# Turning a normalised activation by VectorE and DRAM instead of TensorE, in a two-layer graph network on one core

## The chip, the cores and the metric

The kernel runs on one NeuronCore of a Trainium2 chip. The metric is the device time of one execution in microseconds. One core has five engines with queues of their own: TensorE (PE in the profile; its weight loads are listed apart as PEld), VectorE (DVE), ScalarE (ACT), GpSimd (POOL) and SyncE (SP), which here only issues DMAs. [...]

## The reference, cut to what matters

There are 32 graphs of 512 nodes with 512 features and one adjacency matrix for all of them. Layer 0 mixes neighbours and adds the result to x, then normalises. Layer 1 is masked attention with 8 heads, added and normalised again.

```python
# layer 0
mi = einsum('bkd,od->bko', x, Wi);  mj = einsum('bkd,od->bko', x, Wj)
h  = layernorm(x + deg[None, :, None] * (mi + b) + einsum('ij,bjo->bio', a, mj))
# layer 1
q, k, v = (split_heads(h @ W.T + bias) for W, bias in ((Wq, bq), (Wk, bk), (Wv, bv)))
s    = where(adj == 0, -inf, (q @ k.T) / sqrt(64))
attn = softmax(s) @ v
out  = layernorm(h + attn @ Wo.T + bo)
```

All of it is float32. The three products with Wq, Wk and Wv need h with the features on the partitions, while the normalisation of layer 0 needs it with the nodes on the partitions. So h has to be turned once for each graph. This turning is what the change is about.

## The kernel before, in words

**Names.** For graph b, `XT[b]` is x, later h, later the output: four chunks of 128 nodes by 512 features. `XD[b]` is x turned and multiplied by the degree, `AX_T[b]` the gathered neighbours turned, `HT[b]` h turned. `TX`, `TA`, `TH` and `TO` hold sums of quarters of `XD`, `AX_T`, `HT` and of the attention's output `OT`. All of these but `XT` and `OT` are tiles named `big`, of which there are six.

**Products in seven pieces.** Each 512x512x512 product is done by Strassen's scheme (Winograd's form): seven products of quarters, numbered 1 to 7 (L366 to L436). Pieces 1, 2 and 3 take plain quarters of the activation; 5, 6, 7 and 4 take the sums t1, t2, t3 and t4, which GpSimd makes by subtracting (`combos`, L353 to L362). Pieces share a PSUM bank within a group: 1 and 2, then 6, 7 and 4, then 5 and 3. There are five products for a graph: `l0` (two weights, so each piece is double), `v`, `q`, `k`, and `pj`, the output projection. After a piece, ScalarE or VectorE adds the bank's content to where it belongs. Two banks, a and b, are used in turn, so a piece waits until the piece two before it has been taken away.

**Weights.** The weights' quarters come from DRAM into a ring of eight tiles. After each piece the next tile's load is written on SP's queue (L257 to L262). It can be issued only when the piece has freed its tile, and SP does nothing else in the meantime.

**Order of the work.** Everything is written out by hand as lists of pieces. For each graph n there is a list of phase b (the rest of `l0` of graph n mixed with `pj` of graph n-2), phase c (`v`, `q` and part of `k` of graph n) and phase a (gathers of graph n+1 with the rest of `k` of graph n). `by_steps` cuts it into eight steps of equal TensorE cost, by costs written in the code. Ahead of each step's pieces go the scores and the values of the attention of graph n-1 (L441 to L467) and, in every second step, the sums of the softmax. The softmax's own follow-up (reciprocals, scaling) and some partial sums are handed out after the pieces, one for each 1.73 of written cost. Entries of cost zero, as statistics, scalings, loads and combinations, stand in the lists where their instructions are to be written on their engines.

**Normalising and turning h before.** `stats` (VectorE L274, L275, then three small operations of GpSimd, L276 to L278) and `apply` (ScalarE, L281) each take half the nodes. `l0_norm` (L332 to L339) then turns one chunk of 128 nodes: four TensorE transposes into a PSUM tile that is otherwise used for scores, and one ScalarE copy to `HT`. It stands four times in each graph's lists, with a written cost of 0.44.

**Turning x.** From graph 1 on, x isn't turned by TensorE. `load_xa` (L105 to L110) loads x from DRAM with four DMAs whose runs are 32 floats, so that the 32x32 blocks lie where their turned form belongs. `l0_turn` (L320 to L325) then turns the blocks by VectorE's transpose and multiplies by the degree on GpSimd. The tile `xa` exists once.

Of the kernel before, what the change touches and what calls it, by code (L numbers as in the profile page):

```python
# [9 lines left out]
FT = mybir.dt.float32  # L10
# [15 lines left out]
def gnn_attention_kernel(  # L26
# [51 lines left out]
    def work(shape, name, bufs, dtype=FT):  # L78
        return pools.work.tile(shape, dtype, name=name, bufs=bufs)
# [13 lines left out]
    def turn_tile():  # L93


        return sc_tile()[:, 0, :]

    XT, XA, XD, AX_T, HT, MV = {}, {}, {}, {}, {}, {}
    QT, KT, V, OT = {}, {}, {}, {}
    TX, TA, TH, TO = {}, {}, {}, {}  # L100

    def rows(ap):
        return ap.rearrange("(c p) d -> p c d", p=P)
# [228 lines left out]
    def l0_norm(b, ic):  # L332
# [5 lines left out]
            nc.tensor.transpose(pt[:, dc * P:(dc + 1) * P], y[:, dc * P:(dc + 1) * P], ident)  # L338
        nc.scalar.copy(HT[b][:, :, ic * P:(ic + 1) * P], pt.rearrange("p (c i) -> p c i", c=DC))  # L339

    def add_bo(b, half):
        for ic in range(2 * half, 2 * half + 2):
            y = XT[b][:, ic, :]
            nc.gpsimd.tensor_add(y, y, bo_r)


    def quarter(src, j, n):
        return src[:, 2 * j:2 * j + 2, Q * n:Q * n + Q]
# [28 lines left out]
    def piece(kind, b, i, bank):  # L377
        g = GROUP[i]
        first = (kind, b, g) not in OPEN
        if first:  # L380
            OPEN[kind, b, g] = mm_tile(bank)
        pm = OPEN[kind, b, g]
        terms = []
        for name, (quarters, T) in zip(NAMES[kind], sources(kind, b)):
            a = {1: (0, 0), 2: (1, 0), 3: (1, 1)}.get(i)
            terms.append((take((name, i)), quarters(*a) if a else T[:, {5: 0, 6: 1, 7: 2, 4: 3}[i]]))
        for c in range(2):
            for n, (w, t) in enumerate(terms):
                for kc in range(2):
                    cut = slice(c * P, (c + 1) * P)  # L390
                    lhs, rhs = (w[:, kc, cut], t[:, kc, :]) if kind in "qk" else (t[:, kc, cut], w[:, kc, :])

                    nc.tensor.matmul(pm[:, c * Q:(c + 1) * Q], lhs, rhs, start=first,  # L393
                                     stop=(kc == 1 and n == len(terms) - 1), skip_group_check=True)
                    first = False
        prefetch()
        pm = pm.rearrange("p (c i) -> p c i", c=2)
        if i == 1:
            p1 = OPEN[kind, b, "p1"] = work([P, 2, Q], "p1", 3)
            nc.scalar.copy(p1, pm)  # L400
        p1 = OPEN[kind, b, "p1"]
        f, n = {1: (0, 0), 2: (0, 0), 6: (0, 1), 3: (0, 1), 4: (1, 0), 7: (1, 1), 5: (1, 1)}[i]
        if kind in ("l0", "pj"):
            y = XT[b]
            if i == 1:
                for n, f in ((1, 0), (1, 1), (0, 1)):
                    d = quarter(y, n, f)
                    nc.gpsimd.tensor_tensor(d, d, p1, op=OP.add)  # L408
            else:
                d = quarter(y, n, f)  # L410
                nc.vector.tensor_tensor(d, d, pm, op=OP.add)
        elif kind == "v":
            if i == 1:
                V[b] = work([P, NC, D], "v", 2)
            d = quarter(V[b], n, f)
            if i == 2:
                nc.scalar.copy(d, pm)
            elif i in (6, 7, 4):
                nc.vector.tensor_tensor(d, pm, p1, op=OP.add)  # L419
            elif i != 1:  # L420
                nc.vector.tensor_tensor(d, d, pm, op=OP.add)
        else:
            T, bias = (QT, bq_c) if kind == "q" else (KT, bk_c)
            if i != 1 and (b, f) not in T:
                T[b, f] = work([P, 2, N], kind, 3)
            if i in (6, 7):
                nc.vector.tensor_tensor(T[b, f][:, :, Q * n:Q * n + Q], pm, p1, op=OP.add)  # L427
            elif i != 1:
                for c in range(2):
                    d = T[b, f][:, c, Q * n:Q * n + Q]  # L430
                    bc = bias[:, 2 * f + c:2 * f + c + 1]
                    if i == 2:
                        nc.scalar.activation(d, pm[:, c, :], AF.Identity, bias=bc, scale=1.0)
                    else:
                        o = p1[:, c, :] if i == 4 else d
                        nc.vector.scalar_tensor_tensor(d, pm[:, c, :], bc, o, op0=OP.add, op1=OP.add)  # L436


    E, ES, PV, RL = {}, {}, {}, {}
# [71 lines left out]
    def z(f, *a):  # L511
        return (0.0, f, *a)

    def pc(kind, b, i, bank):
        return (2 * PC if kind == "l0" else PC, piece, kind, b, i, bank)

    ORDER = (1, 2, 6, 7, 4, 5, 3)
    ALONE = ((1, "a"), (6, "b"), (2, "a"), (7, "b"), (5, "a"), (4, "b"), (3, "a"))

    def banks(n):  # L520

        return ("a", "b") if n % 2 == 0 else ("b", "a")

    def phase_a(n):

        A, K = banks(n)
        if n == B:
            return [pc("k", n - 1, i, bank) for i, bank in ((6, K), (7, K), (5, A), (4, K), (3, A))]
        xq, aq = lambda j, m: quarter(XD[n], j, m), lambda j, m: quarter(AX_T[n], j, m)
        g = [(GA, l0_gather, n, dc, A) for dc in range(DC)]  # L530
        k = [pc("k", n - 1, i, K) for i in ORDER[2:]]
        res = []
        for i in range(DC):
            res += g[i:i + 1] + k[i:i + 1]
            if n + 1 < B:
                res += [z(load_xa, n + 1, i)]
            if n == 1 and i in (1, 3):
                res += [z(combine, "wo", nc.vector, i // 2)]
            if i == 1:
                res += [z(combos, TX, n, xq, (1,)), z(combos, TA, n, aq, (1,))]  # L540
        return res + [z(combos, TX, n, xq, (2,)), z(combos, TA, n, aq, (2,)), z(base, n, 0),
                      z(combos, TX, n, xq, (3, 4)), z(combos, TA, n, aq, (3, 4)), z(base, n, 1),
                      pc("l0", n, 1, A), k[4]]
# [36 lines left out]
    def phase_b(n):  # L580

        m = n - 2
        if m < 0:
            res = []
            side = [z(add_bo, 0, i) for i in range(2)]
            A, K = banks(n)
            for i, bank in ((2, A), (6, K), (5, A), (7, K), (4, K), (3, A)):
                res.append(pc("l0", n, i, bank))
                if i == 4:
                    res += [z(stats, n, 0)]  # L590
                res += side[:1]
                side = side[1:]
            return res + [z(apply, n, 0), z(stats, n, 1), (TR, l0_norm, n, 0), (TR, l0_norm, n, 1)]
        res = project(m, 1)
        for i in ORDER[1:]:
            res.append(pc("l0", n, i, banks(n)[0]))
            if i == 4:
                res.append(z(stats, n, 0))
            if i == 5:
                res.append(z(stats, m, 0))  # L600
            if i == 3:
                res += [z(stats, n, 1), (TR, l0_norm, n, 1)]
            res += project(m, i)
            if i == 4:
                res.append(z(apply, n, 0))
            if i == 5:
                res.append((TR, l0_norm, n, 0))
            if i in (7, 4):
                res.append(z(add_bo, n - 1, int(i == 4)))
        return res  # L610

    def phase_c(n):

        m = n - 2
        norm = [(TR, l0_norm, n, ic) for ic in range(NC)]
        h = lambda j, i: quarter(HT[n], j, i)
        A, K = banks(n)
        res = [pc("v", n, 1, A)] + ([z(apply, n, 1)] if n else []) + [pc("q", n, 1, K)]
        if m >= 0:
            res += [z(stats, m, 1)]  # L620
        res += [pc("v", n, 2, A), norm[2], norm[3], z(combos, TH, n, h, (1, 2)), pc("k", n, 1, A),
                z(combos, TH, n, h, (3, 4)), pc("q", n, 2, K), pc("k", n, 2, A)]
        side = []
        if n == 0:

            side = [z(graph_forms, 2), None, z(graph_forms, 0), None, z(graph_forms, 1)]
        if m >= 0:
            res += [z(apply, m, 0), z(apply, m, 1), z(store, m)]
        for i in ORDER[2:]:
            for f in pc("q", n, i, K), pc("v", n, i, A):  # L630
                res += [f] + [g for g in side[:1] if g]
                side = side[1:]
            if i == 7 and 0 < n < B - 1:
                res += [z(load_x, n + 1)]
            if n + 1 < B and i != 3:
                res += [z(l0_turn, n + 1, (6, 7, 4, 5).index(i))]
            if i == 5 and n + 1 < B:
                res += [z(ahead, n + 1)]
        return res

# [266 lines left out]
```

## Time and profile before

| | us |
|---|---|
| median of 14 runs | 3837.95 (3834.87 to 3841.58) |
| profiled execution | 3836.23 |
| its span on the core | 3834.4 |
| TensorE busy | 3794.9 (99%) |
| VectorE busy | 2586.8 (67%) |
| GpSimd busy | 1990.8 (52%) |
| ScalarE busy | 1064.0 (28%) |
| DMA engines, mean share in the queue of SP's loads and stores | 43.0% |
| h's transposes on TensorE, L338, x512: busy | 73.5 (mean 276 ns) |
| copies of these on ScalarE, L339, x128: busy | 72.0 (mean 592 ns) |
| VectorE's transposes of x, L324, x124: busy | 85.6 (mean 690 ns) |
| granted TensorE clock, share of full speed | 0.997 |

The span runs from the first to the last instruction in the profile. Busy times of matmuls overlap one another, so the cost of a TensorE instruction in a dense stretch is better read as the distance between starts. The run has 32 graphs, and the steady part repeats every 117.7 us.

### The profile page before, as it was taken

What the parts mean: (1) busy time and instruction counts of PE and PEld (TensorE: products, weight loads), DVE (VectorE), ACT (ScalarE), POOL (GpSimd) and SP (SyncE); (2) the same over time, 40 slices, a digit from 0 to 9 for tenths busy, and PEclk for the clock granted to TensorE, in tenths of its full rate; (3) what the DMA queues carried; (4) which work ended last, traced back from release to release, by engine and by line L of the source; (5) the groups of instructions that cost most, each with busy time, mean ns of one, the idle gap of its engine ahead of it and who ended that gap; (6) DMA issues with size and microseconds to landing.
All of it is one profiled execution on the core that took longest, in us unless ns stands there. A gap on an engine that the chain in (4) does not pass through costs nothing.

```text
span 3834.4 us, 46277 instructions
## 1 busy us (share of the span) xinstructions
PE 3794.9 (99%) x16906; PEld 2593.8 (68%) x16906; DVE 2586.8 (67%) x3520; ACT 1064.0 (28%) x1476; POOL 1990.8 (52%) x1985
## 2 busy tenths in 40 slices
PE   9999999999999999999999999999999999999997
PEld 6666767666667666666666666767676767666663
DVE  4667676666767676666767676676667676666765
ACT  2232232222232223322223322232222232222222
POOL 4555554555545555445555455554555554555523
PEclk9999999999999999999999999999999999999998
DMA  8434444444444344434444443444434444444330
GB/s 254 127 99 130 126 121 124 124 109 122 126 123 129 99 129 122 129 118 114 119 128 121 126 124 105 126 124 124 127 99 129 127 121 125 125 108 122 115 111 29
DMA packets 537798, 466.33 MB, mean 122 GB/s; under 512 B 279008, under 2 KB 375776, under 8 KB 537568
## 3 DMA queue, kind: packets, MB, share of 16 engines
q1 hardware_dynamic: 537312, 462.78, 43.0%
q8 instruction: 138, 2.26, 0.3%
q14 instruction: 92, 0.75, 0.1%
q0 software_dynamic: 256, 0.53, 0.0%
HBM read 421.80 MB, written 41.42 MB: 121 GB/s over the span
## 4 chain that ended last, share of the span: by engine, by line
PE 95%; DVE 3%; DMA 1%; issue 0%; ACT 0%; POOL 0%; SPq 0%; POOLq 0%; DVEq 0%; ACTq 0%
PE mmb L393 30%; PE mma L393 30%; PE sc L445 12%; PE ov L466 12%; PE mmb L310 3%; PE mma L310 3%; PE ov L473 3%; PE sc L338 1%; DVE e L450 1%; DVE rl L488 1%; DVE st L274 0%; ACT sc L449 0%; DVE es L458 0%; PE ov L483 0%; DMA wq<-e 0%
## 5 line engine op out<-in xcount | busy, mean ns | idle before, releaser
L449 ACT ACTIVATE sc<-sc 128x1024 f32<-128x1024 f32 x512 | 492.9, 1007 | 1354.2 <-PE sc L445 1350.0
L450 DVE TENSOR_TENSOR e<-sc,edge 128x1024 f32<-128x1024 f32 x512 | 602.4, 1217 | 374.7 <-ACT sc L449 374.7
L393 PE MATMUL mmb<-ring,big 128*128 128x256 f32 x3144 | 728.5, 380 | 0.2 <-ACT big L339 0.2
L393 PE MATMUL mma<-ring,big 128*128 128x256 f32 x3112 | 721.3, 380 | 2.8 <-DVE v L419 1.1
L393 PEld LDWEIGHTS mmb<-ring,big 128*128 128x128 f32 x3144 | 593.3, 190 | 106.0 <-issue 25.9
L393 PEld LDWEIGHTS mma<-ring,big 128*128 128x128 f32 x3112 | 587.0, 190 | 108.6 <-issue 25.6
L362 POOL TENSOR_TENSOR big<-big 128x512 f32<-128x512 f32 x376 | 524.9, 1424 | 205.5 <-ACT big L316 164.9
L445 PE MATMUL sc<-q,k 64*128 64x512 f32 x2048 | 509.7, 616 | 0.0
L466 PE MATMUL ov<-e,v 128*64 128x512 f32 x2048 | 496.0, 605 | 5.8 <-DVE oT L498 5.7
L488 DVE RECIPROCAL rl<-ov 128x128 f32<-128x128 f32 x512 | 459.2, 927 | 15.4 <-PE ov L473 6.0
L393 PE MATMUL mma<-big,ring 128*128 128x256 f32 x1808 | 434.3, 383 | 1.3 <-DVE k L436 0.2
L393 PE MATMUL mmb<-big,ring 128*128 128x256 f32 x1776 | 427.0, 383 | 2.0 <-DVE k L427 0.8
L276 POOL TENSOR_SCALAR mv<-mv 128x1 f32<-128x1 f32 x256 | 49.5, 193 | 724.1 <-DVE mv L275 713.9
L325 POOL TENSOR_TENSOR big<-big,deg_r 128x512 f32<-128x512 f32 x124 | 157.5, 1270 | 512.3 <-DVE big L324 512.3
L393 PEld LDWEIGHTS mma<-big,ring 128*128 128x128 f32 x1808 | 336.9, 190 | 83.5 <-issue 24.3
L393 PEld LDWEIGHTS mmb<-big,ring 128*128 128x128 f32 x1776 | 330.5, 190 | 84.7 <-issue 26.0
L466 PEld LDWEIGHTS ov<-e,v 128*64 128x64 f32 x2048 | 124.6, 136 | 345.9 <-issue 270.8
L456 POOL TENSOR_TENSOR es<-e 128x1024 f32<-128x1024 f32 x128 | 302.0, 2359 | 76.7 <-PE ov L473 63.7
L458 DVE TENSOR_TENSOR es<-es,e 128x1024 f32<-128x1024 f32 x248 | 319.3, 1288 | 0.0
L445 PEld LDWEIGHTS sc<-q,k 64*128 64x128 f32 x2048 | 176.6, 186 | 208.1 <-issue 208.1
L193 POOL TENSOR_TENSOR xlo<-xh,xhi 128x512 fp32r<-128x512 f32 x128 | 163.5, 1288 | 213.9 <-ACT xhi L192 213.9
L408 POOL TENSOR_TENSOR xh<-xh,p 128x512 f32<-128x512 f32 x186 | 231.9, 1275 | 45.8 <-ACT sc L449 39.0
(147 smaller groups left out, 3702.8 us busy)
## 6 DMA issues: line engine op xcount, KB each, us to landing
ring<-wq SPq DMA_DIRECT2D x160, 256.0 KB, 2.7
ring<-wv SPq DMA_DIRECT2D x160, 256.0 KB, 2.7
ring<-wk SPq DMA_DIRECT2D x160, 256.0 KB, 2.8
ring<-wi SPq DMA_DIRECT2D x155, 256.0 KB, 2.8
ring<-wj SPq DMA_DIRECT2D x155, 256.0 KB, 2.7
ring<-wo SPq DMA_DIRECT2D x155, 256.0 KB, 2.6
xh<-in_x_dram SPq DMA_DIRECT2D x32, 1024.0 KB, 5.4
xa<-in_x_dram SPq DMA_DIRECT2D x124, 256.0 KB, 3.8
```

The source lines that it names most:

```text
L193: nc.gpsimd.tensor_sub(lo, xs, hi.bitcast(FT))
L310: nc.tensor.matmul(pm, parts[w][:, jc, :], adjR[:, jc, :], start=(w == 0 and jc == 0), stop=(w == 1 and jc == NC - 1))
L362: nc.gpsimd.tensor_tensor(dst, p, q, op=OP.subtract)
L393: nc.tensor.matmul(pm[:, c * Q:(c + 1) * Q], lhs, rhs, start=first, stop=(kc == 1 and n == len(terms) - 1), skip_group_check=True)
L408: nc.gpsimd.tensor_tensor(d, d, p1, op=OP.add)
L445: nc.tensor.matmul(ps[:, s, :], KT[b, hp // 2][r, hp % 2, kc * P:(kc + 1) * P], QT[b, hp // 2][r, hp % 2, :], start=True, stop=True)
L449: nc.scalar.activation(ps, ps, AF.Exp, scale=QSCALE)
L450: nc.vector.tensor_tensor(e, ps, edge[:, kc:kc + 1, :].to_broadcast([P, 2, N]), op=OP.mult)
L456: nc.gpsimd.tensor_add(ES[hp], E[0], E[1])
L458: nc.vector.tensor_add(ES[hp], ES[hp], E[half])
L466: nc.tensor.matmul(PV[hp][s * HD:(s + 1) * HD, :], V[b][:, kc, c0:c0 + HD], E[kc][:, s, :], start=(kc == 0), stop=(kc == NC - 1))
L488: nc.vector.reciprocal(rl[:, c], pl[:, c])
```

## The change

For graphs 2 to 31, h is turned in the way x already was. There are two halves of 256 nodes. For each half:

1. `h_store`: ScalarE issues a DMA that writes the normalised half of `XT` to a DRAM tile (two of these in turn);
2. `h_load`: SP issues four DMAs that read it back in runs of 32 floats into the tile `xa`, so that the 32x32 blocks lie in place;
3. `h_turn`: VectorE turns the half's blocks in one instruction, from `xa` into `HT`.

Graphs 0 and 1 keep `l0_norm`. As the tile `xa` now serves x and h, x's loads move from phase a of the graph before to phase c of the graph before, behind pieces 6 and 7 of q and v, and `l0_turn` moves from phase c to phase a, one behind each gather and piece of k. The load of x in plain form stands behind piece 3 now.

The order of the pieces is different. Phase b starts with a piece of `l0`, not of `pj`, and `pj` piece 3 has moved to phase c. In phase c, for graphs 2 to 31, the first pieces are v1, pj3, v2, q1, k1, q2, k2. The rest of q, v and k is done as 5, 3, 6, 7, 4 instead of 6, 7, 4, 5, 3. So the first piece that lands in a quarter is now 5 or 3 where it was 6 or 7, and the additions of `piece` follow this: the first adds the kept product 1 (and the bias), later ones add to what is there. The number of additions is the same.

```diff
+    def h_store(b, half):
+        if half == 0:
+            HR[b] = dram.tile([N, D], FT, name="hd", bufs=2)
+        nc.scalar.dma_start(rows(HR[b])[:, 2 * half:2 * half + 2, :], XT[b][:, 2 * half:2 * half + 2, :])
+
+    def h_load(b, half):
+        if half == 0:
+            HA[b] = work([P, DC, N], "xa", 1).rearrange("p (n c) (d i) -> p n (c d) i", n=2, d=2)
+        src = HR[b].rearrange("(t p) (c q f) -> q p c t f", p=32, q=4, f=32)
+        for q in range(4):
+            nc.sync.dma_start(HA[b][32 * q:32 * q + 32, half].rearrange("p c (t f) -> p c t f", f=32),
+                              src[q][:, :, 8 * half:8 * half + 8, :])
+
+    def h_turn(b, half):
+        if half == 0:
+            HT[b] = big()
+        nc.vector.transpose(HT[b][:, :, Q * half:Q * half + Q], HA[b][:, half])
...
+    LATE = (5, 3, 6, 7, 4)
...
-        k = [pc("k", n - 1, i, K) for i in ORDER[2:]]
+        k = [pc("k", n - 1, i, K) for i in LATE]
         res = []
         for i in range(DC):
-            res += g[i:i + 1] + k[i:i + 1]
-            if n + 1 < B:
-                res += [z(load_xa, n + 1, i)]
+            res += g[i:i + 1] + k[i:i + 1] + [z(l0_turn, n, i)]
...
+        A = banks(n)[0]
+        l0 = {i: pc("l0", n, i, A) for i in ORDER}
+        return [l0[2], *project(m, 1), l0[6], *project(m, 2), l0[7], z(add_bo, n - 1, 0), *project(m, 6), l0[4], z(stats, n, 0),
+                *project(m, 7), z(apply, n, 0), z(h_store, n, 0), l0[5], z(h_load, n, 0), z(add_bo, n - 1, 1), *project(m, 4),
+                l0[3], z(stats, n, 1), z(h_turn, n, 0), *project(m, 5)]
...
+            res = [z(apply, n, 1), z(h_store, n, 1), v[1], *project(m, 3), z(h_load, n, 1), z(stats, m, 0), v[2], z(stats, m, 1),
+                   q[1], k[1], z(apply, m, 0), q[2], z(apply, m, 1), z(store, m), z(h_turn, n, 1),
+                   z(combos, TH, n, h, (1, 2)), z(combos, TH, n, h, (3, 4)), k[2]]
...
+        for i in LATE:
+            for f in q[i], v[i]:
                 res += [f] + [g for g in side[:1] if g]
                 side = side[1:]
-            if i == 7 and 0 < n < B - 1:
+                if i in (6, 7) and 0 < n < B - 1:
+                    res += [z(load_xa, n + 1, 2 * (i == 7) + (f is v[i]))]
+            if i == 3 and 0 < n < B - 1:
                 res += [z(load_x, n + 1)]
-            if n + 1 < B and i != 3:
-                res += [z(l0_turn, n + 1, (6, 7, 4, 5).index(i))]
-            if i == 5 and n + 1 < B:
+            if i == 7 and n + 1 < B:
                 res += [z(ahead, n + 1)]
```

More of the change, by code (lines that the diff above doesn't have):

```diff
@@ L96, in turn_tile @@
         return sc_tile()[:, 0, :]
+    HA, HR = {}, {}
     XT, XA, XD, AX_T, HT, MV = {}, {}, {}, {}, {}, {}
@@ L411, in piece @@
                 nc.vector.tensor_tensor(d, d, pm, op=OP.add)
-        elif kind == "v":
-            if i == 1:
[L414 to L424, printed above, removed]
-                T[b, f] = work([P, 2, N], kind, 3)
[L426 to L436, printed above, removed]
@@ new lines, in piece @@
+        else:
+            new = (kind, b, f, n) not in OPEN
+            OPEN[kind, b, f, n] = True
+            if kind == "v":
+                if i == 1:
+                    V[b] = work([P, NC, D], "v", 2)
+                d = quarter(V[b], n, f)
+                if i == 2:
+                    nc.scalar.copy(d, pm)
+                elif i != 1:
+                    nc.vector.tensor_tensor(d, pm, p1 if new else d, op=OP.add)
+                return
+            T, bias = (QT, bq_c) if kind == "q" else (KT, bk_c)
+            if i == 1:
+                return
+            if (b, f) not in T:
+                T[b, f] = work([P, 2, N], kind, 3)
+            d = T[b, f][:, :, Q * n:Q * n + Q]
+            if i != 2 and not new:
+                nc.vector.tensor_tensor(d, pm, d, op=OP.add)
+                return
+            for c in range(2):
+                bc = bias[:, 2 * f + c:2 * f + c + 1]
+                if i == 2:
+                    nc.scalar.activation(d[:, c], pm[:, c, :], AF.Identity, bias=bc, scale=1.0)
+                else:
+                    nc.vector.scalar_tensor_tensor(d[:, c], pm[:, c, :], bc, p1[:, c, :], op0=OP.add, op1=OP.add)
@@ L527, in phase_a @@
         if n == B:
-            return [pc("k", n - 1, i, bank) for i, bank in ((6, K), (7, K), (5, A), (4, K), (3, A))]
+            return [pc("k", n - 1, i, bank) for i, bank in ((6, K), (5, A), (7, K), (3, A), (4, K))]
         xq, aq = lambda j, m: quarter(XD[n], j, m), lambda j, m: quarter(AX_T[n], j, m)
         g = [(GA, l0_gather, n, dc, A) for dc in range(DC)]
-        k = [pc("k", n - 1, i, K) for i in ORDER[2:]]
+        k = [pc("k", n - 1, i, K) for i in LATE]
         res = []
         for i in range(DC):
-            res += g[i:i + 1] + k[i:i + 1]
-            if n + 1 < B:
-                res += [z(load_xa, n + 1, i)]
+            res += g[i:i + 1] + k[i:i + 1] + [z(l0_turn, n, i)]
             if n == 1 and i in (1, 3):
@@ L593, in phase_b @@
             return res + [z(apply, n, 0), z(stats, n, 1), (TR, l0_norm, n, 0), (TR, l0_norm, n, 1)]
[L594 to L610, printed above, removed]
+        A = banks(n)[0]
[3 more added lines that the diff above has]
+                l0[3], z(stats, n, 1), z(h_turn, n, 0), *project(m, 5)]
     def phase_c(n):
@@ L617, in phase_c @@
         A, K = banks(n)
[L618 to L622, printed above, removed]
+        v, q, k = [{i: pc(kind, n, i, bank) for i in ORDER} for kind, bank in (("v", A), ("q", K), ("k", A))]
+        if m < 0:
+            res = [v[1]] + ([z(apply, n, 1)] if n else []) + [q[1], v[2], norm[2], norm[3], z(combos, TH, n, h, (1, 2)), k[1],
+                                                             z(combos, TH, n, h, (3, 4)), q[2], k[2]]
+        else:
+            res = [z(apply, n, 1), z(h_store, n, 1), v[1], *project(m, 3), z(h_load, n, 1), z(stats, m, 0), v[2], z(stats, m, 1),
+                   q[1], k[1], z(apply, m, 0), q[2], z(apply, m, 1), z(store, m), z(h_turn, n, 1),
+                   z(combos, TH, n, h, (1, 2)), z(combos, TH, n, h, (3, 4)), k[2]]
         side = []
@@ L626, in phase_c @@
             side = [z(graph_forms, 2), None, z(graph_forms, 0), None, z(graph_forms, 1)]
[L627 to L630, printed above, removed]
+        for i in LATE:
+            for f in q[i], v[i]:
                 res += [f] + [g for g in side[:1] if g]
                 side = side[1:]
-            if i == 7 and 0 < n < B - 1:
+                if i in (6, 7) and 0 < n < B - 1:
+                    res += [z(load_xa, n + 1, 2 * (i == 7) + (f is v[i]))]
+            if i == 3 and 0 < n < B - 1:
                 res += [z(load_x, n + 1)]
-            if n + 1 < B and i != 3:
-                res += [z(l0_turn, n + 1, (6, 7, 4, 5).index(i))]
-            if i == 5 and n + 1 < B:
+            if i == 7 and n + 1 < B:
                 res += [z(ahead, n + 1)]
```

## The prediction

> **What bounds the kernel now.** I read the page's busy shares and chain first, then TensorE's timeline over one graph, then VectorE's and GpSimd's around the joints that the change moves, and the DMA issues last. The page:
>
> ```profile
> span 3834.4 us, 46277 instructions
> ...
> PE 3794.9 (99%) x16906; PEld 2593.8 (68%) x16906; DVE 2586.8 (67%) x3520; ACT 1064.0 (28%) x1476; POOL 1990.8 (52%) x1985
> ...
> PE 95%; DVE 3%; DMA 1%; issue 0%; ACT 0%; POOL 0%; SPq 0%; POOLq 0%; DVEq 0%; ACTq 0%
> ```
>
> TensorE is the chain. It never pauses visibly, so what leaves it shortens the run unless a new wait appears. TensorE's timeline (start, duration, line, operation, tiles):
>
> ```profile
> 1913.35 1.89 PE L393 MATMUL mma<-ring,big 128*128 128x256 f32 x8
> 1915.34 1.99 PE L393 MATMUL mmb<-big,ring 128*128 128x256 f32 x8
> 1917.17 1.89 PE L393 MATMUL mma<-ring,big 128*128 128x256 f32 x8
> 1918.90 1.04 PE L338 MATMUL sc<-ident,xh 128*128 128x128 f32 x8
> 1919.78 1.96 PE L393 MATMUL mma<-big,ring 128*128 128x256 f32 x8
> ...
> 2021.05 0.60 PE L338 MATMUL sc<-ident,xh 128*128 128x128 f32 x4
> 2021.48 3.62 PE L393 MATMUL mmb<-ring,big 128*128 128x256 f32 x16
> 2025.03 1.99 PE L445 MATMUL sc<-q,k 64*128 64x512 f32 x8
> 2026.95 1.94 PE L466 MATMUL ov<-e,v 128*64 128x512 f32 x8
> 2028.82 0.66 PE L338 MATMUL sc<-ident,xh 128*128 128x128 f32 x4
> ```
>
> Durations overlap, so starts are to be subtracted: a single piece costs 1.73 us (1917.17 to 1918.90), an l0 piece 3.46 to 3.55, scores 1.92, values 1.87. The L338 transposes cost 0.88, 0.43 and (next start 2029.32) 0.50: 1.81 us a graph. The distance from the transposes at 1903.35 to those at 2021.05 gives the period, 117.70 us. A piece of v to a piece of q at 1913.35 takes 1.99, not 1.73: 0.26 of a hidden wait for a bank. Two q and v starts near 1948 add 0.3 in the same way, where VectorE turns x.
>
> VectorE (three rows) and then GpSimd (one), for scores that start at 1936.87:
>
> ```profile
> 1939.08 2.36 DVE L450 TENSOR_TENSOR e<-sc,edge 128x1024 f32<-128x1024 f32 x2 [0.75 <-ACT sc L449]
> 1941.35 0.70 DVE L324 STREAM_TRANSPOSE big<-xa 128x512 f32<-128x512 f32 x1
> 1942.68 0.88 DVE L436 SCALAR_TENSOR_TENSOR q<-mmb,bq_c,p 128x256 f32<-128x256 f32 x2 [0.63 <-PE mmb L393]
> ```
>
> ```profile
> 1942.13 1.27 POOL L325 TENSOR_TENSOR big<-big,deg_r 128x512 f32<-128x512 f32 x1 [5.14 <-DVE big L324]
> ```
>
> An operation queued behind the two masks e starts 4.48 us after its step's scores; GpSimd follows a transpose's end by 0.08. The DMA table:
>
> ```profile
> xh<-in_x_dram SPq DMA_DIRECT2D x32, 1024.0 KB, 5.4
> xa<-in_x_dram SPq DMA_DIRECT2D x124, 256.0 KB, 3.8
> out_dram<-xh SPq DMA_DIRECT2D x31, 1024.0 KB, 5.2
> ```
>
> [...] no DRAM round trip of this kind is in the trace. [...] with xa alone in flight the engines move about 210 GB/s, about 390 with 2 KB rows.
>
> **The change part by part**, per graph; 30 graphs (2 to 31) take the new way, graphs 0 and 1 keep TensorE's transposes.
>
> Removed: 16 transposes on TensorE, 1.81 us; 30 times is 54.3 us. Four L339 copies on ScalarE (4 x 0.59 = 2.4 us) were hidden.
>
> Added: two stores of 512 KB issued by ScalarE. Nearest rows: the SP store of 1 MB, issue 0.39, landing 5.2; 256 KB stores at the end landed in 2.0; so 512 KB about 3.1 (bounds 2.0 and 5.2). ScalarE's own issue could cost 0.3 to 2.0 (the shortest and longest ring issue on SP); I take 0.4. ScalarE is 28% busy and has just given up 2.4 us.
>
> Two times four loads of 128 KB by SP. xa's issue is 0.59 for twice the size; I keep 0.65 with the gap, 2.6 us for four. Landing of the last: 3.1 (bounds 2.5 and 5, as xa spread 3.5 to 5.0). Both halves move 1 MB at 210 GB/s plus 1 MB stored at 390: 5.0 + 2.7 = 7.7 us of DMA on a share of 0.45, which becomes about 0.5.
>
> Two transposes of 128x1024 on VectorE. 512 elements take 0.70; [...] twice the row is 1.40. I take 1.25.
>
> **First half.** T is the end of l0[4]. The order written by the lists, cut in eight steps, is: pj7; scores, values, sums (1.92+1.78+0.96); l0[5], pj4, l0[3], pj5; scores, values; v1. So v1 comes at T+20.9. Exponentials of that step's scores end 3.1 after they start, T+4.9; two L281 of 0.78 end at T+6.5, with statistics ready at about T+4. Store issued T+6.6, landed T+9.7. SP reaches h_load only behind the ring tiles that l0[5]'s end frees, T+10.1; last landing 10.1+2.0+3.1 = T+15.2. VectorE reaches h_turn at T+15.4 (l0[3]) + 0.61 add + 0.87 reciprocal + 0.61 scale + 1.66 stats = T+19.15. It doesn't wait for the DMA, with 4.0 to spare. It ends at T+20.4: 0.4 ahead of v1. Queued behind h_turn are pj5's addition, tell and the next two masks; a late h would stop these too, and through v1 TensorE itself. Ring tiles queued on SP behind h_load are delayed by about 1 to 2 us, against a lead of eight tiles, at least four l0 pieces or 13.8 us. I take 0 for v1, bounds 0 and 0.5.
>
> **Second half.** Store at about T+21.9, h_load behind pj3, landing at about T+30.5. S is the start of the scores after q2, T+31.4; h_turn stands behind that step's masks and starts at S+4.48, so again the DMA has 5 us. It ends S+5.73, GpSimd's first combination starts S+5.81 and takes 1.27 to 1.42 (L362): S+7.1 to 7.2. TensorE, after scores, values, sums and k2 (4.65+1.83), wants it for q5 at S+6.48. It waits 0.7; bounds 0.3 and 1.2 (turn of 1.40, contention on GpSimd).
>
> Moved: x's four turns and multiplications go into the gathers. VectorE's sum per gather and k piece is 0.87+0.79+0.87+0.63 = 3.2 of 3.57: fits. On GpSimd the last multiplication ends 4.6 after the last gather (it is behind k7's addition), so its combinations are 4.6 late; the chain through p1's additions ends about 24 after that gather and l0[6] needs it at 26: hidden, 2 us left. x and xa are loaded one step earlier than ScalarE or VectorE wants them: xa's last lands 4 us after v7, first used 12 after. Cover gone, each late microsecond would be paid by TensorE. Banks alternate as before. The moves leave the old hidden waits (0.26 + 0.3, and 0.06 at pj2) with no cause I can find; I count half, 0.25, gained (0 to 0.6).
>
> Sum: 1.81 + 0.25 - 0.7 = 1.36 us a graph, 30 x 1.36 = 41 us. Start and end are priced at 0 (3 either way). From the profiled execution's 3836.23 (span 3834.4) that is 3795; from the median 3837.95, 1.7 above it, 3797.
>
> **Rivals.**
> All hidden: VectorE's turn or GpSimd's combination is quicker and q5 doesn't wait: 1.81 + 0.25 to 0.6 is 62 to 72 us, less what small waits remain: about 3780. For it: 5 us of slack on both DMAs. Against: h_turn's place behind the masks is fixed.
> Both joints wait: v1 0.5 and q5 1.2, none of the old waits lost: 1.81 - 1.7 = 0.1 a graph, 3835; halfway, 3818. For it: v1's margin is only 0.4.
> Slower: the first half's way through DRAM. It has 4.4 us to spare at v1; then each microsecond is paid 30 times, and the gain of 1.36 is gone when the trip from store to last landing is 14.4 instead of 8.6. With the store at 5.2 and loads at 9.3, the median landing of the xa loads queued at the very start, h lands at T+23.7, v1 starts at T+25.1, 4.2 late: net 2.8 worse a graph, 3920; midway between the point of decision and this, 3880. Against: in the middle of the run xa lands in 5.0 at most.
> No effect: the L338 transposes stay; excluded by the lists, only 32 of 512 remain.
>
> **How the numbers follow.** Likeliest 0.50, 3797 (3787 to 3812); all hidden 0.20; both joints 0.13; slower 0.17. A measurement of this kernel can tell 0.2%, 7.7 us, from no change. Faster: 0.50 + 0.20 + 0.08 = 0.78; within 0.2%: 0.05; slower 0.17. The range 3776 to 3838 leaves out the slower case and a little of the first rival.
>
> **What would show it.** L338 falls to x32, with ScalarE's L339. TensorE's period is about 116.3. In TensorE's waits, q5's first matmul waits for GpSimd L362, and v1 hardly for VectorE. In SP's waits, h_load waits mostly for the pieces, not the store. I am wrong if v1 waits for the turn by a microsecond or more, if the four loads land later than 7 us, or if new waits for l0[6] or the gathers name GpSimd.

## The result and the profile after

The changed kernel takes 3795.26 us (median; 3792.47 to 3799.64) against 3837.46 before. The ratio is 0.989, with a 95% interval from 0.988 to 0.99: faster by 42 us, where 41 were forecast (3797). Its profiled execution took 3801.05 us, the slowest of the new kernel's runs, with a span of 3799.2.

The page of the changed kernel: span, busy shares, and the chain by engine.

```profile
span 3799.2 us, 46029 instructions
...
PE 3740.7 (98%) x16426; PEld 2553.8 (67%) x16426; DVE 2696.2 (71%) x3580; ACT 992.8 (26%) x1356; POOL 2029.0 (53%) x1985
...
PE 92%; DVE 4%; POOL 1%; ACT 1%; DMA 1%; issue 1%; SPq 0%; DVEq 0%; POOLq 0%; ACTq 0%
```

TensorE is still the chain, but holds 92% of it instead of 95%: GpSimd and more of VectorE have come in. Most of this is the wait at q5 shown next, for in the run without that wait (below) TensorE holds 97%. 480 TensorE instructions are gone, which is 16 for each of 30 graphs; 32 transposes are left in graphs 0 and 1.

TensorE's timeline of the changed kernel (start, duration, line, operation, tiles, and idle time before it in brackets), around the two joints where the turned h is first used:

```profile
1887.30 1.89 PE L413 MATMUL mmb<-ring,big 128*128 128x256 f32 x8
1889.12 1.99 PE L467 MATMUL sc<-q,k 64*128 64x512 f32 x8
1891.04 1.94 PE L488 MATMUL ov<-e,v 128*64 128x512 f32 x8
1892.91 1.99 PE L413 MATMUL mma<-ring,big 128*128 128x256 f32 x8
...
1903.47 1.99 PE L467 MATMUL sc<-q,k 64*128 64x512 f32 x8
1905.38 1.94 PE L488 MATMUL ov<-e,v 128*64 128x512 f32 x8
1907.15 1.03 PE L495 MATMUL ov<-es,ones 128*64 128x512 f32 x4
1908.11 1.99 PE L413 MATMUL mma<-big,ring 128*128 128x256 f32 x8
1910.66 1.99 PE L413 MATMUL mmb<-big,ring 128*128 128x256 f32 x8 [0.55 <-POOL big L382]
```

The piece at 1892.91 is v1: it follows the values without a gap, so the first half of h is there in time. The piece at 1910.66 is q5: it waits for GpSimd's first combination, by about 0.55 us in 29 of the 30 graphs. VectorE's timeline around the same places:

```profile
1889.70 0.68 DVE L275 BATCH_NORM_STATS2 st<-xh 128x6 f32<-128x512 f32 x1
...
1891.39 1.25 DVE L359 STREAM_TRANSPOSE big<-xa 128x1024 f32<-128x1024 f32 x1
1892.56 0.65 DVE L431 TENSOR_TENSOR xh<-xh,mmb 128x512 f32<-128x512 f32 x1
...
1905.68 2.35 DVE L472 TENSOR_TENSOR e<-sc,edge 128x1024 f32<-128x1024 f32 x2 [3.52 <-ACT sc L471]
1907.95 1.24 DVE L359 STREAM_TRANSPOSE big<-xa 128x1024 f32<-128x1024 f32 x1
```

Neither L359, the turn of h, has a wait in brackets: both halves lie ready when VectorE gets to them. The second one starts 4.48 us after the scores at 1903.47, behind the two masks L472, though VectorE had been idle for 3.52 us ahead of them: here it took its instructions in the order written. What SP waited for at h's loads, in the changed kernel's waits (total, times, longest):

```profile
SPq L353 <- DVE xh L431: 6.4, 26, 0.3
SPq L353 <- DMA hd<-xh: 3.3, 4, 1.6
```

SP stood at the store's landing in 4 of 60 cases only. The loads and stores themselves, from the DMA table (KB each, median us from issue to landing):

```profile
hd<-xh ACTq DMA_DIRECT2D x60, 512.0 KB, 2.9
xa<-hd SPq DMA_DIRECT2D x240, 128.0 KB, 3.6
```

The distance from one graph's first gather to the next one's is 116.02 us in most of the run, against 117.64 before. Two such gathers before, and two after:

```profile
1956.15 1.19 PE L310 MATMUL mmb<-adjR,xhi 128*128 128x512 f32 x4
2073.79 1.19 PE L310 MATMUL mma<-adjR,xhi 128*128 128x512 f32 x4
```

```profile
1936.75 1.19 PE L311 MATMUL mmb<-adjR,xhi 128*128 128x512 f32 x4
2052.76 1.21 PE L311 MATMUL mma<-adjR,xhi 128*128 128x512 f32 x4
```

That is 1.62 us less. For 29 of the 30 graphs the gain lies between two first gathers, 47.0 us together; for the last graph it lies in the end of the run. The execution gained less, because the start and the last graph lost some of it (below).

### The profile page after: what moved, and what is told of

Read it like the earlier page. It is cut to its first block, busy times and chain, and to the rows that moved or that the text cites. A ratio compares the mean times of both kernels' runs of the same rounds, so it can differ in the third digit from the quotient of the medians.

```text
span 3799.2 us, 46029 instructions
## 1 busy us (share of the span) xinstructions
PE 3740.7 (98%) x16426; PEld 2553.8 (67%) x16426; DVE 2696.2 (71%) x3580; ACT 992.8 (26%) x1356; POOL 2029.0 (53%) x1985
## 4 chain that ended last, share of the span: by engine, by line
PE 92%; DVE 4%; POOL 1%; ACT 1%; DMA 1%; issue 1%; SPq 0%; DVEq 0%; POOLq 0%; ACTq 0%
PE mma L413 30%; PE mmb L413 30%; PE sc L467 12%; PE ov L488 11%; PE mmb L311 3%; PE mma L311 3%; PE ov L495 2%; DVE e L472 2%; POOL big L382 1%; DVE big L359 1%; ACT sc L471 1%; DVE rl L510 0%; DVE es L480 0%; PE ov L505 0%; DMA wq<-e 0%
## 5 line engine op out<-in xcount | busy, mean ns | idle before, releaser
L472 DVE TENSOR_TENSOR e<-sc,edge 128x1024 f32<-128x1024 f32 x512 | 602.1, 1217 | 262.1 <-ACT sc L471 262.1
L382 POOL TENSOR_TENSOR big<-big 128x512 f32<-128x512 f32 x376 | 508.1, 1380 | 149.7 <-DVE big L359 129.5
L194 POOL TENSOR_TENSOR xlo<-xh,xhi 128x512 fp32r<-128x512 f32 x128 | 214.4, 1685 | 603.8 <-ACT xhi L193 603.8
L480 DVE TENSOR_TENSOR es<-es,e 128x1024 f32<-128x1024 f32 x248 | 358.7, 1446 | 0.0
L326 POOL TENSOR_TENSOR big<-big,deg_r 128x512 f32<-128x512 f32 x124 | 197.1, 1590 | 177.2 <-DVE big L325 177.2
L431 DVE TENSOR_TENSOR xh<-xh,mma 128x512 f32<-128x512 f32 x186 | 125.8, 676 | 197.0 <-PE mma L413 196.4
```

Source lines behind the costliest of these rows:

```text
L194: nc.gpsimd.tensor_sub(lo, xs, hi.bitcast(FT))
L326: nc.gpsimd.tensor_tensor(XD[b][:, dc, :], XD[b][:, dc, :], deg_r, op=OP.mult)
L382: nc.gpsimd.tensor_tensor(dst, p, q, op=OP.subtract)
L472: nc.vector.tensor_tensor(e, ps, edge[:, kc:kc + 1, :].to_broadcast([P, 2, N]), op=OP.mult)
L480: nc.vector.tensor_add(ES[hp], ES[hp], E[half])
```

## The experiments

My theory was that the gain is the time of the transposes that left TensorE; that the new order only makes room for the way through DRAM; and that what is lost again stands at q5, and comes from where VectorE's turn is written, not from DRAM. "Period" is the distance between the first gathers of two graphs. All changes below are to the changed kernel unless another is named.

### Order alone

```diff
-    l0[3], z(stats, n, 1), z(h_turn, n, 0), *project(m, 5)]
+    l0[3], z(stats, n, 1), z(l0_norm, n, 0), z(l0_norm, n, 1), *project(m, 5)]
...
-    ... z(apply, m, 1), z(store, m), z(h_turn, n, 1),
+    ... z(apply, m, 1), z(store, m), z(l0_norm, n, 2), z(l0_norm, n, 3),
```

with `h_store` and `h_load` left out of the lists.

> The changed kernel's order of pieces and moves, but TensorE turns h again: the transposes and ScalarE copies stand where VectorE's turns stood, and nothing goes by way of DRAM. My theory (the gain is the 1.81 us of transposes that left TensorE, the order only makes room): the period goes from the changed kernel's 116.02 to 116.02 + 1.81 - 0.55 (q5's wait on the combination) + 0 to 0.3 (a smaller wait there) = 117.3 to 117.6, so 3828 to 3840 us, about as before. Rival (the order itself, with fewer hidden waits for banks, made most of the gain): 3800 to 3815 us.

Measured: 3843.43 us, 1.0015 times the kernel before (1.0009 to 1.0022). The period is 117.51 in most graphs and 118.4 in seven, which were not followed up. TensorE's waits in this kernel:

```profile
PE mmb L413 <- POOL big L382: 5.2, 15, 0.3
PE mma L413 <- POOL big L382: 4.9, 14, 0.3
```

So the order by itself gains nothing, and the rival falls: without the way through DRAM it is even a little slower than before. The period was as the theory had it; the run came out 3 us above its upper bound. q5 still waits a little, 0.35 us in 29 graphs, because TensorE's transposes stand behind that step's scores too.

### The second half's turn written earlier

```diff
-    q[1], k[1], z(apply, m, 0), q[2], z(apply, m, 1), z(store, m), z(h_turn, n, 1),
+    q[1], k[1], z(h_turn, n, 1), z(apply, m, 0), q[2], z(apply, m, 1), z(store, m),
```

> The changed kernel with one entry moved: VectorE's turn of h's second half is written ahead of q2, so ahead of the next step's masks instead of behind them. Theory (q5 waits 0.55 us a graph for GpSimd's first combination because the turn stands behind the masks, not because of DRAM): h's second half lands at about 8 us after the store, ahead of the masks, the wait vanishes, 30 x 0.55 = 16 us less: 3779 us (3775 to 3784). Rival (the way through DRAM is what is late): VectorE then waits for the load in front of the masks, nothing gained or slower, 3795 to 3810 us.

Measured: 3768.44 us (3767.26 to 3770.32), 0.9816 times the kernel before (0.9803 to 0.983). VectorE's timeline of this kernel, and then TensorE's at the same place:

```profile
1892.17 1.25 DVE L359 STREAM_TRANSPOSE big<-xa 128x1024 f32<-128x1024 f32 x1 [1.95 <-DMA xa<-hd]
1893.74 2.35 DVE L472 TENSOR_TENSOR e<-sc,edge 128x1024 f32<-128x1024 f32 x2 [0.32 <-ACT sc L471]
```

```profile
1896.17 1.99 PE L413 MATMUL mma<-big,ring 128*128 128x256 f32 x8
1898.00 1.89 PE L413 MATMUL mmb<-big,ring 128*128 128x256 f32 x8
```

VectorE now waits 1.95 us for the load, in time that it had nothing else to do in, and the masks behind it still wait for ScalarE, not for VectorE. q5 follows k2 after 1.83 us instead of 2.55, and the piece behind it follows after 1.73 instead of 1.83. These two make up the 0.83 by which the period falls, to 115.19, where the bracket showed 0.55: after the wait q5 starts 0.56 us behind the end of k2 (1908.11 + 1.99 against 1910.66), and without it 0.16 us ahead of that end, so that the overlap of the two pieces was lost too. This version beats both kernels by one moved entry, 69 us under the kernel before and 27 under the changed one. That is 7 us below the range given. The period accounts for 24 of the 27; in the profiled execution the last graph is 6.5 us shorter too, which the theory did not foresee (see the last graph below).

### The first half's loads later

```diff
-    ... l0[5], z(h_load, n, 0), z(add_bo, n - 1, 1), *project(m, 4), l0[3], z(stats, n, 1), ...
+    ... l0[5], z(add_bo, n - 1, 1), *project(m, 4), l0[3], z(h_load, n, 0), z(stats, n, 1), ...
```

> The changed kernel, but SP's loads of h's first half are written behind l0[3]'s ring tiles instead of l0[5]'s, 4.6 us later in the trace. Theory (the first half has about 2.5 us to spare at v1, 2.2 at VectorE's turn and 0.3 behind it; beyond it each microsecond is paid by TensorE in each of 30 graphs): v1 waits 4.6 - 2.5 = 2.1 us, 30 x 2.1 = 63 us more: 3858 us (3840 to 3870), slower than before the change. Rival (4.4 us to spare, as the prediction worked out): 0.2 us a graph, 3801 us.

Measured: 3896.94 us, 1.015 times the kernel before (1.0136 to 1.0164). TensorE's timeline in a typical graph, and VectorE's:

```profile
1940.42 1.94 PE L488 MATMUL ov<-e,v 128*64 128x512 f32 x8
1944.49 1.97 PE L413 MATMUL mma<-ring,big 128*128 128x256 f32 x8 [2.14 <-issue]
```

```profile
1940.59 0.18 DVE L276 BATCH_NORM_AGGREGATE mv<-st 128x2 f32<-128x6 f32 x1
1943.15 1.25 DVE L359 STREAM_TRANSPOSE big<-xa 128x1024 f32<-128x1024 f32 x1 [2.38 <-DMA xa<-hd]
```

Here v1 waits (the profile calls it issue; VectorE's row shows what it is: the turn behind the load). Counted from the store's issue, the loads go out 5.2 us later than in the changed kernel, not 4.6, and v1 waits 2.5 us in the mean of 29 graphs (2.14 in this one). So the margin of the changed kernel at v1 is about 2.7 us, near the 2.5 assumed here, and not 4.4. But the whole cost is 102 us, where 63 were expected. TensorE's waits marked issue add up to 78.8 us, of which the changed kernel has 3.1 already; the rest is a lower clock after them. In one of these graphs, in a table of stretches (length, busy time of PE, PEld, DVE, ACT and POOL with counts, granted clock, DMA share, GB/s):

```profile
2536.00:2546.00 10.00, 7.27 (x27) 4.33 (x24) 6.96 (x11) 4.04 (x5) 2.00 (x6) 0.83 0.51 125
2546.00:2556.00 10.00, 10.00 (x47) 7.40 (x47) 4.97 (x12) 5.00 (x9) 4.01 (x12) 1.00 0.77 191
```

The clock granted in the stretch with the wait is 0.83, and over the whole run 0.988 against 0.995 in the changed kernel. A loss of 1.2% of 3899.8 us is 47 us, one of 0.5% of 3799.2 is 19; with these 28 us the 75.7 us of added waits come to 104, close to the 102. In some graphs the eight matmuls of v1 then take 3.6 us, in others 1.97 (the last section compares two).

With the loads behind pj4 instead:

> The same loads written behind pj4's ring tiles, 1.2 us later in the trace than in the changed kernel. Theory (2.5 us to spare): hidden, 3795 us (3790 to 3800), with h's landing nearer to VectorE's turn. Rival (the way through DRAM is already on the chain, the margin is nil): 30 x 1.2 = 36 us more, 3831 us.

Measured: 3796.41 us, the same as the changed kernel, with the same waits. In this trace the loads went out 1.7 us later, not 1.2, and the last of them still landed about 1 us ahead of VectorE's turn, against 2.3 in the changed kernel (medians of 30 graphs). A delay of 1.7 us is hidden, one of 5.2 is not.

### The way through DRAM alone, in the old order

```diff
-    res += [z(stats, n, 1), (TR, l0_norm, n, 1)]
+    res += [z(stats, n, 1), z(h_turn, n, 0)]
...
-    res.append((TR, l0_norm, n, 0))
+    res.append(z(h_load, n, 0))
...
-    res += [pc("v", n, 2, A), norm[2], norm[3], z(combos, TH, n, h, (1, 2)), pc("k", n, 1, A),
-            z(combos, TH, n, h, (3, 4)), pc("q", n, 2, K), pc("k", n, 2, A)]
+    res += [pc("v", n, 2, A), pc("q", n, 2, K), pc("k", n, 1, A), pc("k", n, 2, A), z(h_turn, n, 1),
+            z(combos, TH, n, h, (1, 2)), z(combos, TH, n, h, (3, 4))]
```

> The kernel before, in its own order of pieces, with h turned by way of DRAM and VectorE. As its tile for x is taken at that time, h has a tile of its own for each half, and to make room the ring has seven tiles, not eight. The first half's turn stands where l0_norm of chunk 1 stood; the second half's, which would stand after v2, is put off as far as the old order allows, behind k2 and ahead of its combinations. Theory (the new order is what gives the way through DRAM its time): the second half is ready for q6 only about 2.6 us after TensorE gets there (store 3.1, four loads 3.4 + 3.8, turn 1.25, two combinations 2.7, against five pieces and one set of scores, values and sums), and v2 and k1 now wait for a bank about 0.6, so 30 x (-1.81 + 3.2) = 42 us more: 3880 us (3840 to 3930). Rival (the order isn't needed): 3784 to 3800 us.

Measured: 3985.04 us, 1.0381 times the kernel before (1.0366 to 1.0397), worse than the range. TensorE's timeline:

```profile
2105.90 1.97 PE L412 MATMUL mmb<-ring,big 128*128 128x256 f32 x8 [1.75 <-issue]
...
2124.49 2.46 PE L412 MATMUL mma<-big,ring 128*128 128x256 f32 x8 [3.16 <-POOL big L381]
2126.74 3.16 PE L412 MATMUL mmb<-ring,big 128*128 128x256 f32 x8
```

The wait for the second half was 3.16 us, near the 2.6 expected. I had not counted two things: v1 waits 1.75 as well, and after 3.16 us of waiting two pieces run slowly, 5.25 us from start to start where two take 3.46. The sum, -1.81 + 1.75 + 3.16 + 1.8, is 4.9, and the period rose by 5.0. DRAM itself is not what TensorE waits for here: of the 60 turns only one waited for its loads, by 0.4 us. The turns come late because of what stands ahead of them on VectorE, the masks among it, and q6 needs two of GpSimd's combinations behind the turn where q5 needs one. The loads of the second half were only 1.0 us ahead of the turn, however (median), so an earlier turn would have met them. The ring is also one tile shorter in this kernel, but no row names the ring as what TensorE waits for.

### The moved turns of x alone

The kernel before, with its own order of pieces and TensorE's transposes:

```diff
-    res += g[i:i + 1] + k[i:i + 1]
-    if n + 1 < B:
-        res += [z(load_xa, n + 1, i)]
+    res += g[i:i + 1] + k[i:i + 1] + [z(l0_turn, n, i)]
...
+    if i in (6, 7) and 0 < n < B - 1:
+        res += [z(load_xa, n + 1, 2 * (i == 7) + (f[2] == "v"))]
...
-    if n + 1 < B and i != 3:
-        res += [z(l0_turn, n + 1, (6, 7, 4, 5).index(i))]
```

> The kernel before in its own order of pieces, TensorE still turning h; only x's turns are moved from phase c into the gathers of phase a, and its loads in 32-float runs to phase c behind q6, v6, q7 and v7. Theory (the hidden waits of the kernel before near q5 and v5, 0.3 us, come from x's turns on VectorE among the additions of q and v; the 0.26 at q1 and 0.06 at pj2 belong to the order of pieces): the period falls from 117.64 to 117.3, 3828 us (3824 to 3833). Rival 1 (all 0.64 belongs to the moved turns): 3819 us. Rival 2 (none does, GpSimd's later sums cost more in phase a): 3838 us or more.

Measured: 3864.7 us, 1.0068 times the kernel before (1.0055 to 1.0082), with a period of 118.52. TensorE's timeline:

```profile
2010.36 1.94 PE L466 MATMUL ov<-e,v 128*64 128x512 f32 x8
2013.37 1.99 PE L393 MATMUL mma<-ring,big 128*128 128x256 f32 x8 [1.08 <-POOL big L362]
```

The second rival was nearest. The small waits at q5 and v5 have gone as expected, but the piece at 2013.37, pj6, now waits 1.08 us for GpSimd's combination of OT: this is GpSimd's lateness of some 4.6 us after the gathers, which the prediction found and called hidden. It is hidden only because the new order starts phase b with l0[2] and l0[6] and leaves pj6 behind l0[7]. The run of the order alone has the same moves in the new order, and no such wait. In the old order it costs about 1.2 us, and -0.3 + 1.2 gives the 0.88 that the period rose by. So the moves and the order belong together.

### The last graph, and the first half by TensorE

In the last graph the lists are shorter, the steps are cut elsewhere, and no scores stand between l0[3] and v1. TensorE's timeline of the changed kernel there:

```profile
3612.35 5.41 PE L413 MATMUL mmb<-ring,big 128*128 128x256 f32 x16 [2.19 <-DVE xh L431]
...
3637.88 1.89 PE L413 MATMUL mma<-ring,big 128*128 128x256 f32 x8
3642.86 2.92 PE L413 MATMUL mmb<-ring,big 128*128 128x256 f32 x8 [3.09 <-issue]
3645.57 2.67 PE L413 MATMUL mma<-ring,oT 128*128 128x256 f32 x8
```

From the last graph's first gather to the end the changed kernel takes 237.1 us, the kernel before 231.3, though there are 1.8 us of transposes less. Two waits with slow pieces behind them are the difference: from 3608.27 to 3617.69 two pieces take 9.4 us where the steady part takes 5.3 for them, and from 3637.88 to 3648.17 three pieces take 10.3 instead of 5.3. The first wait is for an addition of VectorE that stands behind a sum of 6.08 us, shown in the last section. It doesn't come from the way through DRAM: the run of the order alone has the same sum (6.07 us) and the same wait (2.18), and the run with the second turn earlier has neither, which is most of why its last graph is shorter. The second wait, of v1 at 3642.86, comes from where the turn stands on VectorE, behind l0[3]'s addition and the statistics; the clock is half for 3.41 us behind it. It was tried on top of the earlier second turn:

```diff
-    l0[3], z(stats, n, 1), z(h_turn, n, 0), *project(m, 5)]
+    *([z(h_turn, n, 0)] if n == B - 1 else []), l0[3], z(stats, n, 1),
+    *([] if n == B - 1 else [z(h_turn, n, 0)]), *project(m, 5)]
```

> The kernel with the second half's turn ahead of q2, and in the last graph alone the first half's turn written ahead of l0[3] too. In that graph the steps are cut elsewhere, no scores stand between l0[3] and v1, and in the trace v1 waits 3.1 us there and TensorE runs at a lower clock for some 5 us after it. Theory: this wait goes, with the slow pieces behind it, 5 us: 3763 us (3760 to 3767). Rival (v1 there waits for something else, such as its load or its store): 3768 us, no change.

Measured: 3767.49 us (3763.21 to 3774.66). In its profiled execution that wait is gone and the end takes 228.1 us, 2.6 less than with the second turn alone. The medians of the two don't tell them apart, as this one's runs spread over 11 us. The wait is explained; a gain in time is not shown.

In the last run TensorE turned the first half of h again, with the second half's turn early and by way of DRAM:

```diff
-    l0[3], z(stats, n, 1), z(h_turn, n, 0), *project(m, 5)]
+    l0[3], z(stats, n, 1), z(l0_norm, n, 0), z(l0_norm, n, 1), *project(m, 5)]
```

> The kernel with the second half's turn ahead of q2, but TensorE turns the first half of h again, where VectorE's turn stood; only the second half goes by way of DRAM. Theory (what is left of the gain is the transposes alone and adds up by halves): 8 transposes are 0.91 us a graph, 30 x 0.91 = 27 us more, less some 5 us that v1 no longer waits in the last graph: 3790 us (3785 to 3797). Rival (the first half's trip through DRAM costs TensorE time that the trace doesn't name): less than 3780 us.

Measured: 3797.04 us (3795.14 to 3798.94), at the upper end of the range, and a period of 116.07: 0.88 above the version with both halves through DRAM, 0.91 being the price of eight transposes. So the price adds up by halves, and the first half's trip through DRAM costs TensorE nothing beside what the trace names. In about one graph of six the period is 0.9 longer, which I did not follow up.

## Why the prediction was right

**The transposes.** 1.81 us a graph was the price. The first half alone costs 0.88 more when TensorE does it, half of 1.81 being 0.91. This step holds.

**The first half.** Counted from the end of l0[4] (1872.10 in the trace), v1 was put at 20.9 and came at 20.81; VectorE's turn at 19.15 and came at 19.29; the store's issue at 6.6 and came at 6.37. What was off is the loads: the four issues took 3.4 us, not 2.6, the first of them was issued at 10.7, not 10.1, and a load landed 3.6 us after its issue, not 3.1. So the last one landed at 17.0 (median of 30 graphs), not 15.2, and the margin at v1 was 2.6 us, not 4.4. The run with later loads gives 2.7. The conclusion, no wait at v1, stood in 29 graphs. In the last graph it failed: the prediction cut one graph's list for all 30.

**The second half.** The turn was put 4.48 us after the scores, GpSimd 5.81 after, and came at 4.48 and 5.87. q5 was to wait 0.7. It waits 0.55 in the bracket, and taking it away gained 0.83 of the period. Right in cause and place, a little small in size.

**The old hidden waits.** 0.25 was taken as the half of 0.62. With the wait at q5 gone the period is 115.19, which is 117.64 - 1.81 - 0.64: they go whole. This term was mis-sized, by 0.39.

**The sum.** Foreseen: 1.81 + 0.25 - 0.7 = 1.36 a graph, 41 us. Measured in the period: 1.81 + 0.64 - 0.83 = 1.62, which would be 48.6 us for 30 graphs. The two misses, 0.39 and 0.13, partly cancel.

**Start and end at 0.** This step failed, and its failure is why the total nevertheless came out at 42. In the profiled execution the end, with the last graph's own gain in it, lost 5.8 us, and 47.0 - 5.8 is 41.2. So the range was met by the right mechanism, but that 42 stands so close to 41 is luck: a gain a graph that was put too low and a loss at the end that was put at nothing offset each other. The start, from the first gather of graph 0 to that of graph 1, took 78.0 us against 73.3, and makes this execution slower than the median. TensorE waits 3.03 us in it for a copy by ScalarE, with half clock behind it (0.50 from 63.14 to 69.97 us). In the kernels tried on top of the changed one, which have the same start, this wait was from nothing to 3.72 us and the start took from 71.9 to 78.0, among them 73.5 and 71.9 in the last two runs above. The instructions up to this wait are the same before and after, so nothing shows that the loss at the start is the change's; what makes it vary stays open.

**The rivals.** All hidden was the state that one moved entry then reached: 3768, below the 3780 given for it, since the old waits went whole. The slower one was a real mechanism. The run with later loads reached it with a delay of about 5 us, and it cost more than was worked out, since TensorE was slower behind many of its waits of two to three microseconds (eight matmuls in up to 3.75 us, at 866.38, where others took 1.97). The prediction priced a wait at its length only.

**The store and the turn.** SP's wait for the store is 3.3 us over the whole run. The prediction held that the trace before has no such trip through DRAM; it has one at the start, where combined weights are stored (`wq<-e`) and read back, and SP waits 3.6 us for that store. The 1.25 us for the turn of 1024 elements was an estimate of the author's, between the 0.70 measured for 512 and twice that; the trace's mean is 1.24.

## What to carry to other kernels

When an engine that bounds the kernel hands work to another, list for each consumer what stands ahead of the new instruction on its new engine, not only whether its data is there: here the data was ready and the instruction stood behind two masks, and moving its entry ahead of them gained another 27 us, 24 of them in the period. A long way (store, load, turn) is free as long as the order gives it time (a delay of 1.7 us was hidden here, one of 5.2 cost 102 us), so the way and the order have to be tried together; here each part tried without the others was slower than before, if only a little (by 0.15%, 0.7% and 3.8%). Check the first and last rounds of a loop by themselves, as work that hides a latency in the middle may be missing there (v1 waited 3.09 us in the last graph alone).

## What the runs showed of the hardware that I had not expected

These are readings of the profiles of these runs.

Some waits of TensorE cost more than their length. Behind waits of 2.5 us (loads behind l0[3]) and 3.2 us (the way alone, in the old order) eight matmuls took up to 3.6 us instead of 1.97; around one such wait the granted clock was 0.83 over ten microseconds. A wait of 2.15 us was already followed by slow matmuls (2.94 us), while others of 2.34 and even 3.20 us were not.

So the length alone doesn't decide. In the traces of the kernel before and of the changed one the record of the granted clock has only two values, full and half, and within each of the two runs the changes between them lie whole multiples of 3.41 us apart (63.14, 69.97, 3613.00, 3616.42 us and so on in the changed kernel). The wait of 2.15 us that was followed by slow matmuls (first three rows) and the one of 3.20 us that was not, both in the run with the loads behind l0[3], look like this in stretches of that length (columns as in the table of stretches above):

```profile
384.26:387.68 3.42, 1.27 (x6) 0.80 (x5) 2.19 (x3) 1.19 (x2) 0.49 (x2) 1.00 0.77 227
387.68:391.09 3.41, 3.41 (x10) 2.67 (x9) 3.41 (x5) 0.58 (x1) 0.00 (x0) 0.50 0.18 44
391.09:394.50 3.41, 3.41 (x17) 3.00 (x17) 2.48 (x4) 0.52 (x1) 0.00 (x0) 1.00 0.56 154
742.67:746.08 3.41, 1.49 (x8) 0.29 (x4) 0.07 (x1) 2.26 (x3) 1.29 (x5) 1.00 0.71 158
746.08:749.50 3.42, 2.14 (x10) 1.95 (x11) 3.42 (x6) 0.14 (x1) 0.00 (x0) 1.00 0.41 153
749.50:752.91 3.41, 3.41 (x18) 2.93 (x17) 3.41 (x5) 0.54 (x2) 0.00 (x0) 1.00 0.47 120
```

The shorter wait lies whole in one stretch, which leaves TensorE idle for 2.15 us of it, and the next stretch is granted half clock. The longer one is divided by such a point into 1.92 and 1.28 us, and the clock stays full. The kernel before and the changed one agree: cut at the points of their own changes, they have some 2200 stretches at full clock, counted from where the record of the clock starts (12 to 13 us into the span). The eight of these in which TensorE was idle for 2.03 us or more were each followed by half clock, and none of the others was, with idle times up to 1.87 us. That one belongs to a wait of 2.54 us at 3672.60 in the kernel before, which such a point divides, and the eight matmuls behind it took 1.94 us. As an estimate from the 3.41 us, such a stretch at half the clock does the work of 1.7 us where TensorE is busy throughout, and so adds about 1.7 us to the wait. What sets the clock in this way was not shown.

VectorE's partial sum of 1024 elements took 1.22 us in the median of both kernels. In the changed kernel it took 2.56 us in one place of a typical graph, and 6.08 in the last graph:

```profile
1867.80 2.56 DVE L480 TENSOR_TENSOR es<-es,e 128x1024 f32<-128x1024 f32 x1
3605.62 6.08 DVE L480 TENSOR_TENSOR es<-es,e 128x1024 f32<-128x1024 f32 x1
```

Beside the first GpSimd ran two additions, from 1866.77 to 1869.27, and beside the second three subtractions and two additions without a pause, from 3604.46 to 3610.61. Both sums ended 1.09 us after the last of these. So it is with all 61 of these sums that took over 1.5 us in this kernel: each ended 1.08 or 1.09 us after an instruction of GpSimd, which is not far from the 1.22 us of a whole sum. No run here was made to show the cause. On average this sum went from 1.29 to 1.45 us, and with the moved turns of x alone it is 1.45 as well. GpSimd's split of x went from 1.29 to 1.69; with the moved turns alone it stays at 1.30, and with the new order it is 1.66 without any way through DRAM, so that it belongs to the order of the pieces.
